# Reordering TensorE's work in a four-layer attention kernel: scores three steps ahead, values in fours, context transposes chained, products held back

## The chip, the cores and the metric

The kernel runs on one core of one Trainium2 chip. The metric is the device time of one execution in microseconds (us). A core has five engines that each work through a queue of their own in order: TensorE (PE in the profile, with its weight loads shown apart as PEld), VectorE (DVE), ScalarE (ACT), GpSimd (POOL) and SyncE (SP), which here issues transfers. They wait for each other through semaphores. TensorE writes into PSUM, eight banks of 2 KB per partition, and the other engines move results on into SBUF. Everything here is 32-bit floating point.

## The reference

The input x is (8, 112, 256): 8 batches of 112 tokens. The context ctx is (8, 375, 192). Four layers follow each other:

```python
# layers 0 and 1: three sub-blocks, each with its own layer norm and a residual
x = attn(ln(x), ln(x)) + x            # self attention, 16 heads of 64, scale 1/8
x = attn(ln(x), ctx) + x              # cross attention over 375 context rows
x = (a * gelu(gate)) @ Wf + bf + x    # a, gate = split(ln(x) @ Wp + bp); 256 -> 2 x 1024 -> 256
# layer 2: cross attention alone, 16 heads of 64
x = x + (softmax(q @ k.T) * scale) @ v @ Wo + bo
# layer 3: decoder block, 16 heads of 16, masks
x = x + self_attn(ln(x), causal and target mask) @ proj_w + proj_b
x = x + cross_attn(ln(x), ctx, context mask) @ out_w + out_b
x = x + gelu(ln(x) @ mlp1_w + mlp1_b) @ mlp2_w + mlp2_b     # 256 -> 1024 -> 256
```

Layer 1 uses the tanh form of gelu, the others the exact one.

## The kernel before

**Stages.** The sub-blocks are numbered as stages: 0, 1, 2 (layer 0: self, cross, feed forward), 3, 4, 5 (layer 1), 6 (layer 2's cross attention), 7, 8, 9 (layer 3: self, cross, feed forward). The 896 tokens lie in seven tiles of 128 rows. The text speaks of three blocks, which the code calls segments 0, 1 and 2: stages 0–2, 3–5 and 6–9. The last block is stage 8 with what is woven into it, and the feed forward behind it (stage 9).

**Steps.** Attention is cut into steps (`add_step`, L913). A self step of stages 0 and 3 takes one batch and 8 of its heads; a cross step one batch and 4 heads; a self step of stage 7 one batch and 8 heads of 16. The 16 self steps of stage 7 are not a run of their own: a dictionary `after` weaves them in pairs between the cross steps of stages 6 and 8. Each step has up to four parts:

- S (`emit_s`): the scores, matmuls at L986 into a PSUM tile `s`. The pool `ps_s` (L313) has two such tiles of two banks each; a cross step and a self step of stage 7 take both, a self step of stages 0 and 3 takes one. The softmax is issued with it. For heads of 64: a maximum on VectorE (L948), one exp per head on ScalarE (L954), a reciprocal (L960, L967) and a scaling on GpSimd (L963 for cross steps, one instruction per head; L969 for self steps). For heads of 16: one VectorE instruction per head adds the mask, copies the scores from PSUM into the SBUF tile `pr` and takes the maximum `nm` (L934); the exps on ScalarE work in `pr` (L942), with the sums collected and divided out once per batch (R and N, L1082–1091).
- E (`emit_late`): for heads of 16, half of the exps are issued with S and the other half here, later in ScalarE's queue.
- T (`emit_t`): transposes of `pr` on TensorE (L1013) into a PSUM tile `mm` (the pool `ps_m`, L314, has four of one bank each), two groups for a self step of 64, three for a cross step (chunks of 128, 128 and 119 context rows). Each group is copied to an SBUF tile `wT`: by ScalarE (L1022) or, for the middle group, VectorE (L1019) in stages 7 and 8; by whichever of the two has less planned load (`evac`, L331; L347 is ScalarE, L355 VectorE) elsewhere.
- PV (`emit_pv`): the values (L1043), accumulated in an `mm` tile that is copied to `oT` (L1054 or `evac`).

**Fillers.** Everything else on TensorE is a filler with a cost and a deadline, counted in steps: key projections (L791 with L800), value projections (L825 with L834; L866 with L875 in stage 8; L750 for self steps), query projections (L703, L725), transposes of the normalized x into `hT` (L637, copied at L642 or by `evac`), products with the output weights (L669, then the residual on VectorE at L673), the transposes of the context into `ctxA` and `ctxB` (L897, six transposes, two copies and one transfer per batch), the feed forward (L1263 in stages 2 and 5, L1298 in stage 9). The class `Plan` keeps them with their dependencies, each with a gap in planned microseconds, and with the room that their results need in SBUF (`arena`, 12224 elements per partition, and rings of weight tiles). `pace` says how much filler work a step must take so that all deadlines are met, `fill` takes the ready one with the earliest deadline, `main` issues a part of a step, `open_jobs` starts a key or value job whose matmul opens early and whose end (`begin` and `fn`) comes in the next step.

**Order.** TensorE's queue is in the order in which the program issues (`manual_schedule` for PE alone); the other engines' order comes from the scheduler, except where `keep_in_program_order` fixes it. So the main loop (L1454–1495) writes TensorE's order out: in step i it issues S(i+2); on every second step PV(i−1) and PV(i); then fillers; the T groups of step i+1 with fillers between them; E(i+2); and fillers again.

**The feed forward at the end.** `last_ff` (L1281) cuts the tokens into 512, 256 and 128 columns (f = 0, 1, 2), with eight products m each. For f = 0 each product (2 matmuls of 512 columns, L1298) has the deadline `ready + 4 + m` in steps, so that they are spread over the last cross steps; their bias is added on the way out of PSUM, and two Gelu instructions over all of them (L1325) come when all eight are there and the last S lies back. For f = 1 VectorE adds the bias (L1309), for f = 2 ScalarE takes bias and Gelu together. Before the first Gelu ScalarE loads another function table (ACT_TABLE_LOAD in the profile). The products L669 of `add_products` with the last weights end the kernel.

Of the kernel before, what the change touches and what calls it, by code (L numbers as in the profile page):

```python
# [299 lines left out]
def kernel(ctx: ExitStack, tc: tile.TileContext, a: dict, out: bass.AP):  # L300
# [3 lines left out]
    ARENA = 12224  # L304
# [4 lines left out]
    ppool = ctx.enter_context(tc.tile_pool(name="ppool", bufs=4))  # L309
    tpool = ctx.enter_context(tc.tile_pool(name="tpool", bufs=6))  # L310
# [235 lines left out]
    def add_masks():  # L546
# [18 lines left out]
        plan.add(Item(("mask", "self"), 0, self_mask, first_of(7, 0) - 8, uses=[src], seg=SEG[6]))  # L565
        yield
        for i in range(2):
            key = ("w", "cm", i)

            def place(i=i, key=key):  # L570
                got[key] = wpool.tile([T, 4, S], F32, tag="w", name="cm")

            plan.add_load(Item(("load", key), 0, place, makes=[key]))
            for n in range(4):

                def ctx_mask(i=i, n=n, key=key):
                    c = B * T + (4 * i + n) * S
                    nc.gpsimd.tensor_scalar_mul(got[key][:, n, :], got[src][:, c : c + S], NEG)

                b = 4 * i + n  # L580
                plan.add(Item(("mask", b), 0, ctx_mask, first_of(8, b) - 5, uses=[src, key], seg=SEG[7]))
# [305 lines left out]
    def add_context_transposes(deadline):  # L887
        for b in range(B):
# [15 lines left out]
            plan.add(Item(("ctxT", b), 0.7, fn, deadline(b), uses=[key], deps=[(("S", 2 + b // 3), 2.0)]))  # L904
# [275 lines left out]
    def q_deadline(st, j):  # L1180
        return first_of(st, 2 * j) - 3.4
# [27 lines left out]
    def hT_by(st):  # L1209
# [4 lines left out]
        return lambda gi: first_of(st, (256 * gi) // T) - 4  # L1214
# [22 lines left out]
    def cross_stage(st, wq, wk, wv, qscale, vscale):  # L1237
# [6 lines left out]
        for b in range(B):  # L1244

            add_key_jobs(st, b, wk, lambda b, u: at[(st, b, u)] - 3.0, last)
# [40 lines left out]
    def last_ff(st, w1, bias):  # L1287
# [3 lines left out]
        for f, (lo, n) in enumerate(LASTG):  # L1291
            ready = last_of(8, last_batch(tiles_of(lo, lo + n)[-1]))
            for m in range(8):

                def fn(f=f, lo=lo, n=n, m=m):
# [12 lines left out]
                    else:  # L1308
                        tc.keep_in_program_order(nc.scalar.activation(dst, ps[:, :n], AF.Gelu, bias=col(bias, m)))  # L1309

                plan.add(
                    Item(
                        ("ff", st, f, m), 8 * n / 2400, fn, ready + (4 + m, 2.5 + 0.2 * m, 5 + 0.1 * m)[f],
                        uses=[w1],
                        deps=h_deps(st, lo, lo + n) + [(("norm", st, t), 0) for t in tiles_of(lo, lo + n)]
                        + ([(("gelu", st, 1), 0)] if f == 2 else []),
# [136 lines left out]

    cuts = [0, ff_at[2], ff_at[5], ff_at[9]]  # L1454
    for seg in range(3):
# [12 lines left out]
        if seg == 0:  # L1468
            plan.require(("hT", 0, 1))
        for i in range(lo - 2, hi):  # L1470
# [6 lines left out]
            if lo <= i + 2 < hi:  # L1477
                plan.main(("S", i + 2))

            if lo <= i < hi and (i - lo) % 2 == 1:  # L1480
                plan.main(("PV", i - 1))
                plan.main(("PV", i))
# [7 lines left out]
            if ("E", i + 2) in plan.items and lo <= i + 2 < hi:  # L1490
                plan.main(("E", i + 2))
# [42 lines left out]
```

## Time and profile before

| what | value |
|---|---|
| median of 3 runs | 1653.15 us (1653.11 to 1653.16) |
| the profiled execution | 1654.93 us |
| its span in the profile | 1653.1 us |
| granted TensorE clock, mean | 0.999 |
| TensorE busy | 1633.3 us in 11772 instructions |
| VectorE, ScalarE, GpSimd busy | 812.8, 782.6, 718.5 us |
| read from HBM, mean over the span | 35.88 MB, 22 GB/s |

A line of the timeline has its start and its duration in us, the engine, the line of the kernel, the operation, result and operand names, the tile sizes, the number of instructions in the group, and in brackets how long the engine stood idle before it and which engine's result ended that wait. A line of the waits has the waiting engine, result and line, the engine, result and line waited for, the total in us, the number of waits and the longest. TensorE's instructions overlap: a matmul's record is longer than the distance to the next one's start, so its busy time is not a measure of how well it is used.

### The profile page before, as it was taken

The numbers are of one execution on the slowest core, as the hardware profiler recorded it, in microseconds if no ns is written. First come the engines' busy times: TensorE is split into PE (matmuls) and PEld (weight loads), VectorE is DVE, ScalarE is ACT, GpSimd is POOL, SyncE is SP. The second block draws the span as 40 slices with busy tenths as digits, with TensorE's granted clock in tenths as the row PEclk, the third lists the DMA queues.
The fourth block names the chain that finished last, engine by engine and source line by source line (L and its number), as shares of the span: only waits on it lengthen the run. The fifth ranks groups of instructions, "written<-read, shape, count | busy, mean of one in ns | idle before, by whom it ended". The sixth has DMA issues, their size and how long they took to land.

```text
span 1653.1 us, 30104 instructions
## 1 busy us (share of the span) xinstructions
PE 1633.3 (99%) x11772; PEld 1141.0 (69%) x11772; DVE 812.8 (49%) x2164; ACT 782.6 (47%) x2450; POOL 718.5 (43%) x687
## 2 busy tenths in 40 slices
PE   9999999999999999999999999999999999999999
PEld 8777766666657878676666665675666666766667
DVE  3554454544532344545444552344455556677752
ACT  3453444444531445434444452144445555787772
POOL 1323555656632223355565570364564447422110
PEclk9999999999999999999999999999999999999999
DMA  6021020000101011000000010100000000000000
GB/s 187 5 66 42 3 87 1 1 26 1 52 29 46 1 29 52 27 1 30 1 2 26 1 46 30 33 23 1 1 2 1 16 2 26 30 2 1 2 2 23
DMA packets 26613, 39.50 MB, mean 24 GB/s; under 512 B 1527, under 2 KB 21623, under 8 KB 26471
## 3 DMA queue, kind: packets, MB, share of 16 engines
q1 hardware_dynamic: 26231, 37.40, 7.3%
q8 instruction: 93, 1.52, 0.4%
q14 instruction: 49, 0.40, 0.1%
q10 hardware_dynamic: 240, 0.17, 0.0%
HBM read 35.88 MB, written 0.92 MB: 22 GB/s over the span
## 4 chain that ended last, share of the span: by engine, by line
PE 91%; ACT 4%; DVE 3%; POOL 1%; issue 1%; ACTq 0%; POOLq 0%; DVEq 0%
PE mm L669 13%; PE mm L703 11%; PE mm L1043 10%; PE s L986 10%; PE mm L1013 9%; PE mm L791 8%; PE mm L825 7%; PE mm L1263 6%; PE mm L800 5%; PE mm L834 4%; PE mm L750 3%; ACT pr L942 2%; PE mm L1298 2%; PE mm L637 1%; ACT pr L954 1%
## 5 line engine op out<-in xcount | busy, mean ns | idle before, releaser
L963 POOL TENSOR_SCALAR pr<-pr,rinv 112x375 f32<-112x375 f32 x384 | 468.7, 1239 | 340.6 <-DVE rinv L960 340.6
L954 ACT ACTIVATE pr<-s,nm 112x375 f32<-112x375 f32 (+1 forms) x640 | 302.0, 490 | 168.7 <-DVE nm L948 166.5
L355 DVE COPY arena<-mm 128x375 f32<-128x375 f32 (+4 forms) x189 | 113.3, 609 | 287.8 <-PE mm L800 138.3
L1013 PEld LDWEIGHTS mm<-ident,pr 112*128 112x128 f32 (+2 forms) x1920 | 209.1, 151 | 48.1 <-issue 20.6
L1013 PE MATMUL mm<-ident,pr 112*128 112x112 f32 (+2 forms) x1920 | 234.7, 264 | 5.5 <-ACT pr L942 3.3
L347 ACT COPY arena<-mm 128x375 f32<-128x375 f32 (+4 forms) x179 | 92.8, 519 | 296.3 <-PE mm L800 140.9
L948 DVE TENSOR_REDUCE nm<-s 112x2 f32<-112x750 f32 (+1 forms) x224 | 206.3, 957 | 50.2 <-PE s L986 46.5
L986 PE MATMUL s<-arena 64*112 64x375 f32 (+3 forms) x1792 | 211.0, 394 | 0.1
L1043 PEld LDWEIGHTS mm<-wT,arena 128*64 128x64 f32 (+5 forms) x3840 | 160.5, 130 | 36.9 <-issue 19.0
L347 ACT COPY wT<-mm 119x448 f32<-119x448 f32 (+2 forms) x235 | 123.9, 536 | 124.5 <-PE mm L1013 124.4
L1043 PE MATMUL mm<-wT,arena 128*64 128x112 f32 (+5 forms) x3840 | 180.3, 262 | 0.0
L986 PEld LDWEIGHTS s<-arena 64*112 64x112 f32 (+1 forms) x1792 | 114.1, 172 | 80.4 <-issue 30.9
L942 ACT ACTIVATE pr<-pr,nm 112x112 f32<-112x112 f32 (+1 forms) x256 | 124.7, 491 | 32.0 <-DVE nm L934 32.0
L969 POOL TENSOR_TENSOR pr<-pr,rinv 112x896 f32<-112x896 f32 x32 | 53.9, 1685 | 197.5 <-DVE rinv L967 180.0
L954 ACT ACTIVATION_READ_ACCUMULATOR pr<-s,nm 112x1 f32 x640 | 133.3, 208 | 0.0
L599 POOL TENSOR_TENSOR rs<-ve,mhalf 128x1 f32<-128x1 f32 x70 | 39.7, 568 | 203.0 <-DVE ve L597 202.9
L960 DVE RECIPROCAL rinv<-sums 112x1 f32<-112x1 f32 x384 | 62.4, 163 | 90.1 <-ACT pr L954 89.6
L825 PE MATMUL mm<-L_xattn_Wv,ctxA 128*128 128x512 f32 (+1 forms) x192 | 92.5, 601 | 2.3 <-ACT wT L347 1.3
L791 PE MATMUL mm<-ctxA,L_xattn_Wk 128*128 128x375 f32 x256 | 92.0, 482 | 0.6 <-DVE wT L355 0.5
L673 DVE TENSOR_TENSOR x<-mm,x 128x256 f32<-128x256 f32 x70 | 29.6, 423 | 115.9 <-PE mm L669 115.9
L703 PE MATMUL mm<-hT,L_xattn_Wq 128*128 128x224 f32 x384 | 83.0, 360 | 0.0
L353 DVE TENSOR_SCALAR arena<-mm 128x448 f32<-128x448 f32 (+2 forms) x65 | 42.0, 646 | 82.0 <-PE mm L834 47.1
(134 smaller groups left out, 2323.7 us busy)
## 6 DMA issues: line engine op xcount, KB each, us to landing
L_xattn_Wo<-in_L_xattn_Wo_dram SPq DMA_DIRECT2D x3, 1024.0 KB, 15.8
L_xattn_w_ff<-in_L_xattn_w_ff_dram SPq DMA_DIRECT2D x3, 1024.0 KB, 5.2
L_xattn_Wv<-in_L_xattn_Wv_dram SPq DMA_DIRECT2D x4, 512.0 KB, 5.0
L_xattn_Wq<-in_L_xattn_Wq_dram SPq DMA_DIRECT2D x2, 1024.0 KB, 4.7
L_xattn_Wp<-in_L_xattn_Wp_dram SPq DMA_DIRECT2D x2, 1024.0 KB, 5.8
L_xattn_wq<-in_L_xattn_wq_dram SPq DMA_DIRECT2D x2, 1024.0 KB
L_xattn_wo<-in_L_xattn_wo_dram SPq DMA_DIRECT2D x2, 1024.0 KB, 5.2
L_xattn_mlp_w<-in_L_xattn_mlp_w_dram SPq DMA_DIRECT2D x2, 1024.0 KB, 5.4
```

The source lines that it names most:

```text
L347: nc.scalar.copy(dst, src)
L669: nc.tensor.matmul(ps[:, :D], lhsT=oT[:, c, t * P : (t + 1) * P], rhs=got[wv or w][:, c, :], start=(c == 0), stop=(c == n - 1),)
L703: nc.tensor.matmul(ps[:, i * 2 * T : (i + 1) * 2 * T], lhsT=got[w][:, k, m * P : (m + 1) * P], rhs=hT[:, k, lo:hi], start=(k == 0), stop=( ...
L791: nc.tensor.matmul(ps[:, :S], lhsT=got[wv][:, (2 * u + i) * P : (2 * u + i + 1) * P], rhs=ctxA[:, cols], start=True, stop=False,)
L825: nc.tensor.matmul(ps[: KCH[c][1], :], lhsT=lhs(ctxA, slice(0, KA), c), rhs=got[w][:, hf * 512 : (hf + 1) * 512], start=True, stop=False,)
L942: return nc.scalar.activation(pr, pr, AF.Exp, bias=nm, scale=-1.0, accum_out=bsums[(st, b)][:, h : h + 1])
L948: nc.vector.tensor_reduce(nm[:, :, :ns], sv, AX.X, ALU.max, negate=True)
L954: nc.scalar.activation(pr[:, bk, sl, :], sv[:, bk, sl, :], AF.Exp, bias=nm[:, bk, sl : sl + 1], accum_out=sums[:, bk, sl : sl + 1],)
L963: nc.gpsimd.tensor_scalar_mul(pr[:, bk, sl, :], pr[:, bk, sl, :], rinv[:, bk, sl : sl + 1])
L986: nc.tensor.matmul(tiles[i][:, n % 2, (n // 2) * nk : (n // 2 + 1) * nk], lhsT=qap(h), rhs=kap(h), start=True, stop=True,)
L1013: nc.tensor.transpose(pt[:kl, m * T : (m + 1) * T], cell[h][:, c * P : c * P + kl], ident[:T, :T])
L1043: nc.tensor.matmul(po[p0 : p0 + dp, blk * T : (blk + 1) * T], lhsT=got[vk][:kl, hv * dp : (hv + 1) * dp], rhs=wt, start=(c == 0 and par(h) ...
```

## The change

Seven things change, all of them in the order and place of instructions:

- The loop keeps a list of S parts that are due. From step `DEEP` on, three steps before the first cross step of stage 8, S is issued three steps ahead in place of two, and E with it. At the step where it begins two S parts follow each other.
- PV parts wait in a list. In segments 0 and 1, for the 16 self steps, they are issued four together on every fourth step; elsewhere two together as before.
- The context transposes of batch b depend on those of batch b − 1, with a gap of 1.5 planned us.
- In `last_ff`, the products m = 5, 6, 7 of f = 0 depend on the last S and get deadlines of `len(steps) − 3` to `len(steps) − 1`.
- The pools of `pr` and `wT` tiles grow from 4 to 6 and from 6 to 8, the arena shrinks from 12224 to 9536 elements.
- Masks are due a step earlier.
- Queries and `hT` of stages 7 and 8, and keys of stage 8, are due a step earlier.

```diff
@@ -301,13 +301,13 @@
     nc = tc.nc
     PSUM = bass.MemoryType.PSUM
     RINGS = {"w": 7, "row": 2, "xn": 3}
-    ARENA = 12224
+    ARENA = 9536
 
     const = ctx.enter_context(tc.tile_pool(name="const", bufs=1))
     wpool = ctx.enter_context(tc.tile_pool(name="wpool", bufs=RINGS["w"]))
     rpool = ctx.enter_context(tc.tile_pool(name="rpool", bufs=RINGS["row"]))
-    ppool = ctx.enter_context(tc.tile_pool(name="ppool", bufs=4))
-    tpool = ctx.enter_context(tc.tile_pool(name="tpool", bufs=6))
+    ppool = ctx.enter_context(tc.tile_pool(name="ppool", bufs=6))
+    tpool = ctx.enter_context(tc.tile_pool(name="tpool", bufs=8))
     xpool = ctx.enter_context(tc.tile_pool(name="xpool", bufs=RINGS["xn"]))
     small = ctx.enter_context(tc.tile_pool(name="small", bufs=4))
     ps_s = ctx.enter_context(tc.tile_pool(name="ps_s", bufs=2, space=PSUM))
@@ -562,7 +562,7 @@
             )
 
         plan.add_load(Item(("load", "masks"), 0, load, makes=[src]))
-        plan.add(Item(("mask", "self"), 0, self_mask, first_of(7, 0) - 8, uses=[src], seg=SEG[6]))
+        plan.add(Item(("mask", "self"), 0, self_mask, first_of(7, 0) - 9, uses=[src], seg=SEG[6]))
         yield
         for i in range(2):
             key = ("w", "cm", i)
@@ -578,7 +578,7 @@
                     nc.gpsimd.tensor_scalar_mul(got[key][:, n, :], got[src][:, c : c + S], NEG)
 
                 b = 4 * i + n
-                plan.add(Item(("mask", b), 0, ctx_mask, first_of(8, b) - 5, uses=[src, key], seg=SEG[7]))
+                plan.add(Item(("mask", b), 0, ctx_mask, first_of(8, b) - 6, uses=[src, key], seg=SEG[7]))
 
 
     xns = {}
@@ -901,7 +901,7 @@
                     evac(dst[:kl, cols], pc[:kl, :S], S)
                 nc.sync.dma_start(ctxB[KB:, cols], ctxB[:KB, cols])
 
-            plan.add(Item(("ctxT", b), 0.7, fn, deadline(b), uses=[key], deps=[(("S", 2 + b // 3), 2.0)]))
+            plan.add(Item(("ctxT", b), 0.7, fn, deadline(b), uses=[key], deps=[(("S", 2 + b // 3), 2.0)] + [(("ctxT", c), 1.5) for c in range(b - 1, b) if b]))
 
 
 
@@ -1178,7 +1178,7 @@
         return lambda t: [(("N", st, last_batch(t)), 1.2)]
 
     def q_deadline(st, j):
-        return first_of(st, 2 * j) - 3.4
+        return first_of(st, 2 * j) - (4.4 if st > 6 else 3.4)
 
     L0 = ("L0_xattn_", "Wq1 Wk1 Wv1 Wo1 bo1 g1 b1 Wq2 Wk2 Wv2 Wo2 bo2 g2 b2 Wp Wf bf g3 b3 bp".split())
     L1 = (
@@ -1211,7 +1211,7 @@
             return lambda gi: last_of(8, last_batch(GROUPS[gi][-1])) + 2.0
         if st in ff_at:
             return lambda gi: ff_at[st] - 0.5 + 0.02 * gi
-        return lambda gi: first_of(st, (256 * gi) // T) - 4
+        return lambda gi: first_of(st, (256 * gi) // T) - (5 if st > 6 else 4)
 
     def norm_by(st):
         f = hT_by(st)
@@ -1243,7 +1243,7 @@
                 add_pair_projection(st, "q", j, wq, 4, lambda j, u: q_deadline(st, j) + 0.01 * u, qscale)
         for b in range(B):
 
-            add_key_jobs(st, b, wk, lambda b, u: at[(st, b, u)] - 3.0, last)
+            add_key_jobs(st, b, wk, lambda b, u: at[(st, b, u)] - (4.0 if last else 3.0), last)
             if not last:
                 add_value_jobs(st, b, wv, lambda b, i: at[(st, b, (0, 0, 2)[i])] - 1.5 + 0.1 * i, vscale)
 
@@ -1308,12 +1308,17 @@
                     else:
                         tc.keep_in_program_order(nc.scalar.activation(dst, ps[:, :n], AF.Gelu, bias=col(bias, m)))
 
+
+
+                held = f == 0 and m > 4
                 plan.add(
                     Item(
-                        ("ff", st, f, m), 8 * n / 2400, fn, ready + (4 + m, 2.5 + 0.2 * m, 5 + 0.1 * m)[f],
+                        ("ff", st, f, m), 8 * n / 2400, fn,
+                        len(steps) - 8.0 + m if held else ready + (4 + m, 2.5 + 0.2 * m, 5 + 0.1 * m)[f],
                         uses=[w1],
                         deps=h_deps(st, lo, lo + n) + [(("norm", st, t), 0) for t in tiles_of(lo, lo + n)]
-                        + ([(("gelu", st, 1), 0)] if f == 2 else []),
+                        + ([(("gelu", st, 1), 0)] if f == 2 else [])
+                        + ([(("S", len(steps) - 1), 0)] if held else []),
                         seg=SEG[st],
                     )
                 )
@@ -1451,6 +1456,7 @@
     nc.vector.tensor_copy(vcols, pt0[:, :NVR])
     plan.now = 7.0
 
+    DEEP = first_of(8, 0) - 3
     cuts = [0, ff_at[2], ff_at[5], ff_at[9]]
     for seg in range(3):
         lo, hi = cuts[seg], cuts[seg + 1]
@@ -1467,6 +1473,7 @@
                     plan.drain(mk)
         if seg == 0:
             plan.require(("hT", 0, 1))
+        waiting = []
         for i in range(lo - 2, hi):
             plan.step = i
             left = plan.pace(i, seg)
@@ -1474,12 +1481,20 @@
 
                 left = max(left, 6.5)
             plan.close_jobs()
-            if lo <= i + 2 < hi:
-                plan.main(("S", i + 2))
-
-            if lo <= i < hi and (i - lo) % 2 == 1:
-                plan.main(("PV", i - 1))
-                plan.main(("PV", i))
+
+
+            ahead = 3 if seg == 2 and i >= DEEP else 2
+            due = [n for n in range(i + 2, i + ahead + 1) if lo <= n < hi and not plan.items[("S", n)].done]
+            for n in due:
+                plan.main(("S", n))
+
+
+            if lo <= i < hi:
+                waiting.append(("PV", i))
+                full = 4 if seg < 2 and i < lo + 16 else 2
+                if len(waiting) == full:
+                    while waiting:
+                        plan.main(waiting.pop(0))
             if lo <= i + 1 < hi:
                 n = steps[i + 1]
                 share = left / (n + 2)
@@ -1487,8 +1502,9 @@
                 for k in range(n):
                     plan.main(("T", i + 1, k))
                     left -= plan.fill(min(left, share))
-            if ("E", i + 2) in plan.items and lo <= i + 2 < hi:
-                plan.main(("E", i + 2))
+            for n in due:
+                if ("E", n) in plan.items:
+                    plan.main(("E", n))
             plan.fill(left, 1.5 if i < lo else 0.0)
 
 
```

## The prediction

> **What bounds the kernel now.** I read the page first, then busy time by stretches, then TensorE's timeline row by row in the last block, then what it waited for, and last the timelines of the engines named there. The page:
>
> ```profile
> PE 1633.3 (99%) x11772; PEld 1141.0 (69%) x11772; DVE 812.8 (49%) x2164; ACT 782.6 (47%) x2450; POOL 718.5 (43%) x687
> ```
>
> TensorE bounds everything, but 99% hides losses: matmul records overlap. Stretches 1400–1600 and 1600–1653 (columns: length, then busy time of PE, PEld, DVE, ACT, POOL, granted clock, DMA share):
>
> ```profile
> 1400.00:1600.00 200.00, 194.06 (x2069) 132.62 (x2068) 144.65 (x565) 148.00 (x477) 54.42 (x82) 1.00 0.03 8
> 1600.00:1653.00 53.00, 47.43 (x334) 40.10 (x331) 17.64 (x51) 18.42 (x39) 5.43 (x7) 0.97 0.06 18
> ```
>
> In the last block TensorE is idle 5.9 of 200 us, the most of any stretch, and ScalarE is busy 148 (74%): the runner-up. TensorE's timeline from the second-last cross step to the feed forward:
>
> ```profile
> 1598.87 0.90 PE L986 MATMUL s<-arena 32*112 32x375 f32 x8
> 1599.70 0.41 PE L1089 MATMUL mm<-ident,rb 112*128 112x112 f32 x2
> 1599.94 0.58 PE L1013 MATMUL mm<-ident,pr 112*128 112x112 f32 x3
> 1600.80 1.12 PE L1013 MATMUL mm<-ident,pr 112*128 112x112 f32 x9 [0.28 <-ACT pr L942]
> 1602.40 1.13 PE L669 MATMUL mm<-squares,oT 128*128 128x256 f32 x4 [0.48 <-ACT wT L1022]
> 1603.46 0.90 PE L986 MATMUL s<-arena 32*112 32x375 f32 x8
> 1604.29 1.36 PE L1043 MATMUL mm<-wT,arena 128*32 128x112 f32 x48
> 1605.59 1.40 PE L1013 MATMUL mm<-ident,pr 112*128 112x112 f32 x12
> ...
> 1613.77 7.20 PE L1298 MATMUL mm<-hT,L_xattn_mlp_w 128*128 128x256 f32 x32 [0.64 <-DVE hT L642]
> ```
>
> Starts tell more than durations. Three transposes from 1599.94 at one per 0.096 us (the x12 group of a quiet step, 1551.19 to 1552.49, gives 0.1) would let the next start at 1600.23; it starts at 1600.80. The printed idle of 0.28 is thus a loss of about 0.57, since the pipe drains and refills. I count every wait by starts. The scores S (L986) are followed too closely by the transposes T of the step before, which need its exps. Waits of TensorE, by cause:
>
> ```profile
> PE mm L1013 <- ACT pr L942: 3.3, 10, 0.7
> ...
> PE mm L791 <- ACT wT L1022: 1.1, 2, 0.6
> ```
>
> ScalarE at the end (exps, copies and Gelu share one queue), GpSimd at the start of the woven steps, and VectorE on a self step's mask and maximum:
>
> ```profile
> 1601.83 0.94 ACT L1022 COPY wT<-mm 128x448 f32<-128x448 f32 x2
> ...
> 1610.63 1.28 ACT L1325 ACT_TABLE_LOAD   x1
> 1611.92 3.71 ACT L1325 ACTIVATE oT<-oT 128x2048 f32<-128x2048 f32 x2
> ```
>
> ```profile
> 1401.27 4.90 POOL L963 TENSOR_SCALAR pr<-pr,rinv 112x375 f32<-112x375 f32 x4
> 1406.11 0.31 POOL L770 MEMSET arena<- 112x256 f32 x1
> 1406.40 4.88 POOL L963 TENSOR_SCALAR pr<-pr,rinv 112x375 f32<-112x375 f32 x4
> ```
>
> ```profile
> 1409.13 0.28 DVE L934 CUSTOM_DVE_ANT_0 pr<-s,cmask 112x112 f32<-112x112 f32 x1 [0.86 <-PE s L986]
> ```
>
> The eighth of these starts at 1410.49 and its accumulator read at 1410.69: 0.195 us each. The span is 1653.1 and the execution 1654.93, 1.8 outside the span and 1.8 above the median 1653.15. I sum against the execution and shift the median by the sum.
>
> **The change, part by part.** No arithmetic is added or removed: every instruction of before is there again in another place, so TensorE's pure work stays and only waits, and changes of tile shape, move. I set TensorE's new instruction order against the old one and laid the rows' start-to-start times along it.
>
> *Values in fours.* Changing TensorE's tile shape costs time: eight S passes run four at a time, 2 x 0.316 = 0.63 by the steps inside the group, but 1603.46 to 1604.29 is 0.83; 48 value passes take 1.14 by their inner steps, but 1604.29 to 1605.59 is 1.30. That is 0.16–0.20 each. The new order has 469 such changes against 478: 9 x 0.18 = −1.6 (ends −0.9 and −1.8). Waits of 0.4–0.6 behind value pairs in block 0 (1-us neighbourhoods of 56.07 and 84.27) mostly go: −0.8 (0 to −1.2). The value outputs only take two PSUM buffers longer together; ppool at 6 and tpool at 8 hold the four steps' tiles, so no buffer wait appears in the order.
>
> *Context transposes* (L897). Each item issues six transposes, two copies and one DMA on SP. Three came in a row with S, a copy and a wait: 169.15 loses 0.63, 214.38 0.90, 237.91 0.85, with restarts 2.75 in all. The copies end 3.5 us after S starts (165.64 to 169.10). The new order spreads the early ones, but three of the S–transposes–T–products groups remain, with 2.84–2.90 us of work where 3.5 is wanted: I take −0.45 (ends 0 and −2.75). Their DMA is 96 kB on a queue whose order is otherwise nearly unchanged, and every weight load is still issued over 17 us ahead: nothing there. If that cover went, the late part of one load (5 us to land) would be the price.
>
> *Masks a step earlier.* Four 1.16-us GpSimd products per half plus 3.5 for the self mask go past an emptier GpSimd (54 of 200 busy): 0; behind them L963 of a cross step would be late by at most 1.2.
>
> *Key and query jobs a step earlier, smaller arena.* In stages 1 and 4, three matmuls that waited 0.40 for a wT copy (3.44 us of work behind an S whose copy is ready 3.84 after it) become key matmuls with 3.22: +0.65 (0 to +1.2). In stage 6 two new waits of the same kind (2.15 us after S: 1.1, and 0.6) come against 1.2 that go: +0.5. There GpSimd too: a step's four scalings take 4.9 us, and the new order puts S's 4.3 and 3.9 us apart in two places, so queueing begins: about 0.6, and 1.6 in place of the 0.35 lost at 1411.33: +1.85. Stage 6 together +2.35 (0 to +4).
>
> *Scores three ahead.* Entry: two S's follow each other directly, the self step's 112-wide and then 375-wide ones, which want the PSUM banks that the eight reduces (8 x 0.195 = 1.56, starting 0.8 after S, 1409.13 against 1408.32) empty: 2.36 after the self S starts, where TensorE is done with it after 0.5. Everything on TensorE queues behind the second S: +1.9 (1.0 to 2.4). Gain: the ten exp waits by starts. Eight before the last S lose 1.12 (near 1460), 0.16, 0.22, 0.82, 0.97, 0.82, 0.54, 0.63 = 5.28. Work between S and its T was 3.4–9 us, a loss where it was under 5, and is now 6–16, mostly 9–12; explicit waits on exps fall from 96 to 8. −5.1 (ends −5.3 and 0).
>
> *What is late next*: the copies of T (L1022). The copies of 1601.83 started when exps queued ahead were out: S 1598.87, wait ended 1602.40, 3.53 later. ScalarE's queue still puts two exps of the new S ahead of the copies. Waits of this kind lose 5.6 us by starts before; the new order has 11 places under 3.3 us with deficits of 4.7, so 0 net, plus 0.4 for restarts within a group (−0.3 to +1.3).
>
> *Held products.* After the last S, TensorE loses 4.05 before (0.37, 0.87, 0.50 at the T's, 0.8 in the values, 1.05 at 1613.77 and the rest small). Three held products, 1.73 each (1566.32 to 1568.05), 5.2 us, fill that. But in ScalarE's queue the table load (1.28) and two Gelus (3.71) now precede three wT copies. With the last S at 0, the first copy ends at 11.0, the Gelus at 16.0, the next copy at 16.5; TensorE wants its PSUM buffer at 14.35: 2.2 lost, 1.05 for hT and the first evacuation, 0.25 restarts: 3.5. Net −0.5 (−4 to +1.5). 1610.63 directly follows the copy that ends at 1610.61: the row shows no wait around the load. The Trainium skill ("ScalarE: Activation LUTs", "What ACT_TABLE_LOAD costs") speaks against the change here: it gives the load about 1283 ns, as the row shows, plus a drain of about 1380 ns, which the rows do not show. By the page the tail would lose 1.4 more and the sum would be −1.8.
>
> Sum: −1.6 −0.8 −0.45 +0.65 +2.35 +1.9 −5.1 +0.4 −0.5 = −3.15 us. Execution 1654.93 to 1651.8, median 1653.15 to 1650.0. A measurement of this kernel tells about 0.2% (3.3 us) from no change.
>
> **The rivals.**
> 1. *The costs are covered.* Entry, GpSimd and Gelu terms (1.9 + 1.85 + about 1) find other work: −3.15 − 4.75 = −7.9, 1645.2. For it: idle GpSimd and VectorE. Against: their waits are on TensorE's own next instruction.
> 2. *Copies take the exps' place.* If exps of the earlier S make copies ready at S + 3.75 rather than 3.53, the 11 places lose about 0.2 each more, with a few new ones 2.5 in all: −0.65, about 1652.5. For it: rows where both waits alternate (1600.80, 1602.40). Against: ScalarE has 26% idle.
> 3. *The lookahead does nothing.* S(i+3) waits for a PSUM tile until its step's reduces are done, and the T waits stay: −3.15 + 5.1 = +1.95, 1655.1. For it: there are only two pairs of score banks. Against: the reduces of the S at 1598.87 have let the first half-exps start by 1600.65, and from S to S lie 4.2 us of work on average.
> 4. *Slower: ScalarE becomes the bound of the last block.* A cross step costs it 4 x 0.59 exps (1600.06 to 1600.65) + 2 x 0.48 copies = 3.3 us against 4.2 of TensorE per step on average, but TensorE's stretches are 1.9–3.3 in about eleven steps. From the point where copies come later than S + 3.9 every step pays, and ScalarE never catches up: 32 x 0.25 = 8.0, and 2 of the 5.1 are lost again: −3.15 + 8.0 + 2 = +6.85, 1660.0. For it: ScalarE's 74% is an average over steps that need 79% (3.3 of 4.2). Against: the last steps, where work is thinnest, still show gaps of 1.51 in its row of exps.
>
> **How the numbers follow.** Forecast 0.35, rival 1 0.20, rival 2 0.12, rival 3 0.08, rival 4 0.25. The forecast's own range is 1647.5 to 1652.5, half of it under 1649.85 where faster begins. Faster: 0.20 + 0.18 = 0.38. Same: 0.17 + 0.12 + 0.07 = 0.36. Slower: 0.25 + 0.01 = 0.26. The range from 1645.0 leaves out half of rival 1 (0.10) and, ending at 1657.5, half of rival 4 (0.12).
>
> **What would show it.** Right: exp waits of L1013 in the last block fall under 1 us; waits on wT by L1022 stay near 5; at the first cross step of the last block S waits for L934's nm for about 1.9; GpSimd's L963 groups join without a gap near 1330 and 1375; after the last S three L1298 512-wide groups, then a wait on wT across the Gelu pair. Wrong: waits on wT well above 6 (rivals 2, 4), or S stalls at every step on nm (rival 3), or no wait at the Gelus (rival 1). A loss in blocks 0 and 1, where I find few new waits, would mean that a queue I costed at nothing was the cover.

## The result and the profile after

| | before | after |
|---|---|---|
| median | 1653.16 us (1653.09 to 1654.79, 6 runs) | 1663.41 us (1661.82 to 1665.41, 6 runs) |
| ratio | | 1.0057, 95% interval 1.0047 to 1.0067 |
| profiled execution, span | 1654.93, 1653.1 us | 1661.82, 1659.4 us |

The change made the kernel 10.25 us slower, where 3.15 us faster was forecast; the range ended at 1657.5. The two profiled executions lie 6.9 us apart and their spans 6.3: the one of before stands 1.8 above its median, the one of after 1.6 below. The six times of the changed kernel fall into two groups, 1661.8 to 1662.0 with a mean granted clock of 0.999 to 1.0, and 1664.8 to 1665.4 with 0.997 to 0.998; the last section comes back to that. The profiled execution of before has a stretch at half clock too, from 1610.28 to 1613.69, which its median has not (columns as in the prediction, the clock third from the end):

```profile
1610.30:1613.60 3.30, 2.83 (x46) 2.10 (x36) 0.70 (x2) 3.27 (x3) 0.00 (x0) 0.50 0.00 0
```

The profiled execution of after has none. At a clock of 1.0 the changed kernel takes 1661.8; the kernel before takes 1652.9 to 1654.4 in the runs beside the experiments. So the change costs 7.4 to 8.9 us at equal clock, and the rest of the 10.25 is clock.

Busy time in the last stretches of the changed kernel (columns as before):

```profile
1400.00:1600.00 200.00, 189.56 (x2009) 130.03 (x2007) 143.47 (x563) 150.72 (x491) 56.65 (x85) 1.00 0.02 8
1600.00:1659.00 59.00, 53.89 (x408) 43.95 (x406) 19.02 (x54) 21.19 (x44) 5.43 (x7) 1.00 0.05 16
```

TensorE is idle 10.4 of 200 us between 1400 and 1600, where it was 5.9. Its waits in the changed kernel:

```profile
PE mm L866 <- ACT wT L1022: 4.7, 5, 2.0
...
PE mm L1298 <- ACT wT L1022: 1.8, 1, 1.8
PE mm L1013 <- POOL pr L963: 1.6, 2, 0.9
...
PE s L986 <- DVE nm L934: 1.1, 1, 1.1
```

One of them in the kernel before:

```profile
PE mm L866 <- ACT wT L1022: 0.7, 3, 0.3
```

The waits of L1013 on the exps of L942, 3.3 us in 10 before, are gone from the list: what the third step was to remove, it removed. In their place stand waits on wT copies, on GpSimd and on the maxima.

Where did the time go? I gave every instruction of TensorE, in its order, its quiet start-to-start distance (0.096 us for 112 columns, 0.216 for 256) and 0.18 per change of tile shape, and subtracted that from the actual starts. What is left over between two points with the same amount of work done is lost time, whether TensorE waited or ran at a lower clock. The stretches are named by the times of before:

| stretch of before, us | lost before | lost after | difference | predicted |
|---|---|---|---|---|
| 0–29 | 2.4 | 2.8 | +0.4 (1.8 to 3.1 in all traces) | 0 |
| 29–111, block 0 | 2.2 | 3.7 | +1.6 | −0.8 |
| 111–272, context transposes | 4.4 | 3.8 | −0.6 | −0.45 |
| 272–931 | 6.5 | 7.6 | +1.1 | +0.65 with the next |
| 931–1223 | 5.3 | 5.1 | −0.2 | |
| 1223–1401, stage 6 | 6.1 | 7.5 | +1.4 | +2.35 |
| 1401–1424, entry | 1.2 | 5.7 | +4.6 | +1.9 |
| 1424–1597, last block | 15.1 | 16.7 | +1.6 | −4.7 |
| 1597 to the end | 5.5 | 3.5 | −2.1 | −0.5 |
| tile shapes, 478 to 469, counted | 84.1 | 82.5 | −1.6 | −1.6 |
| sum | | | +6.3 | −3.15 |

The sum is the difference of the two spans. Between forecast and measurement lie 9.4 us: 6.3 of them in the last block, 2.7 at the entry and 2.4 in block 0, while the tail came out 1.6 better.

But of the 5.5 that the tail loses before, 1.3 is the half-clock stretch. Run 11 below has the same order there at full clock. Before first, then run 11:

```profile
1609.91 2.17 PE L1043 MATMUL mm<-wT,arena 128*32 128x112 f32 x48
1612.02 1.11 PE L637 MATMUL mm<-ident,xn 128*128 128x128 f32 x4
```

```profile
1615.17 1.36 PE L1043 MATMUL mm<-wT,arena 128*32 128x112 f32 x48
1616.47 0.66 PE L637 MATMUL mm<-ident,xn 128*128 128x128 f32 x4
```

By starts the 48 values take 2.11 and 1.30 us, and from L637 to the next L1298 (at 1613.77 and 1617.76) it is 1.75 and 1.29. At equal clock the change gains about 0.8 in the tail, not 2.1.

The entry, TensorE's timeline and GpSimd's in the changed kernel:

```profile
1401.51 1.43 PE L986 MATMUL s<-arena 64*112 64x375 f32 x8
...
1405.64 0.89 PE L986 MATMUL s<-arena 64*112 64x375 f32 x4 [0.22 <-ACT pr L954]
1406.76 0.89 PE L986 MATMUL s<-arena 64*112 64x375 f32 x4 [0.22 <-ACT pr L954]
...
1415.40 0.32 PE L1013 MATMUL mm<-ident,pr 112*128 112x112 f32 x1 [0.90 <-POOL pr L963]
...
1418.89 0.66 PE L986 MATMUL s<-arena 32*112 32x112 f32 x16
1420.62 1.66 PE L986 MATMUL s<-arena 32*112 32x375 f32 x8 [1.06 <-DVE nm L934]
```

```profile
1405.34 4.90 POOL L963 TENSOR_SCALAR pr<-pr,rinv 112x375 f32<-112x375 f32 x4 [1.40 <-DVE rinv L960]
1410.18 0.31 POOL L770 MEMSET arena<- 112x256 f32 x1
1410.47 4.88 POOL L963 TENSOR_SCALAR pr<-pr,rinv 112x375 f32<-112x375 f32 x4
```

The same two S parts before:

```profile
1395.53 1.52 PE L986 MATMUL s<-arena 64*112 64x375 f32 x8
...
1403.01 1.43 PE L986 MATMUL s<-arena 64*112 64x375 f32 x8
```

They lay 7.5 us apart; now, at 1401.51 and 1405.64, it is 4.1. The second has to wait for the exps of the first; GpSimd, which needs 4.9 us for each, ends at 1415.4, and TensorE waits for that. The double S at 1418.89 and 1420.62 comes on top.

Two self steps and a cross step in the last block, TensorE and ScalarE:

```profile
1498.07 0.66 PE L986 MATMUL s<-arena 32*112 32x112 f32 x16
...
1501.29 0.75 PE L986 MATMUL s<-arena 32*112 32x112 f32 x16
...
1505.77 1.13 PE L866 MATMUL mm<-ctx_w,ctxA 128*128 128x256 f32 x4 [1.96 <-ACT wT L1022]
```

```profile
1501.38 0.94 ACT L1022 COPY wT<-mm 128x448 f32<-128x448 f32 x2
...
1505.20 0.94 ACT L1022 COPY wT<-mm 128x448 f32<-128x448 f32 x2
```

Between the copies lie eight exps of a self step, 0.37 us each, one behind the other without a gap. TensorE has the next S 3.2 us after the last one, and ScalarE needs about 3.8 for eight exps and two copies.

Block 0 and the tail of the changed kernel:

```profile
54.65 0.48 PE L897 MATMUL mm<-ident,cn 125*128 125x125 f32 x3
55.58 0.51 PE L897 MATMUL mm<-ident,cn 125*64 125x125 f32 x3 [0.46 <-DVE arena L355]
56.53 0.19 PE L410 MATMUL mm<-ident,brows 8*128 8x8 f32 x1 [0.44 <-PE mm L897]
...
63.67 0.44 PE L637 MATMUL mm<-ident,xn 128*128 128x128 f32 x2 [0.78 <-DVE arena L355]
```

```profile
1613.98 1.28 ACT L1330 ACT_TABLE_LOAD   x1
1615.27 3.71 ACT L1330 ACTIVATE oT<-oT 128x2048 f32<-128x2048 f32 x2
1618.89 1.38 ACT L1022 COPY wT<-mm 119x448 f32<-119x448 f32 x3
```

```profile
1616.96 0.67 PE L1013 MATMUL mm<-ident,pr 112*119 112x112 f32 x4 [0.58 <-DVE oT L1307]
1619.45 3.72 PE L1298 MATMUL mm<-hT,L_xattn_mlp_w 128*128 128x256 f32 x16 [1.82 <-ACT wT L1022]
```

Values in fours leave room in block 0, the plan fills it with a context transpose 22 us earlier than before (54.65 against 76.9), at a place where VectorE has a maximum and four copies from PSUM to do one after the other (53.85 to 56.96). In the tail three copies stand behind the Gelus, as the prediction had it.

### The profile page after: what moved, and what is told of

It reads as the page before. It is cut to its first block, busy times and chain, and to the rows that moved or that the text cites. A ratio compares the mean times of both kernels' runs of the same rounds, so it can differ in the third digit from the quotient of the medians.

```text
span 1659.4 us, 30169 instructions
## 1 busy us (share of the span) xinstructions
PE 1631.8 (98%) x11772; PEld 1141.4 (69%) x11772; DVE 816.6 (49%) x2160; ACT 783.7 (47%) x2454; POOL 718.3 (43%) x687
## 4 chain that ended last, share of the span: by engine, by line
PE 90%; ACT 4%; DVE 3%; POOL 1%; issue 1%; ACTq 0%; DVEq 0%; POOLq 0%
PE mm L669 12%; PE mm L703 11%; PE mm L1043 10%; PE s L986 10%; PE mm L1013 9%; PE mm L791 8%; PE mm L825 7%; PE mm L1263 6%; PE mm L800 5%; PE mm L834 4%; PE mm L750 3%; ACT pr L942 2%; PE mm L1298 1%; ACT pr L954 1%; PE mm L725 1%; DVE pr L934 1%
## 5 line engine op out<-in xcount | busy, mean ns | idle before, releaser
L1013 PEld LDWEIGHTS mm<-ident,pr 112*128 112x128 f32 (+2 forms) x1920 | 208.7, 151 | 45.1 <-issue 20.5
L1013 PE MATMUL mm<-ident,pr 112*128 112x112 f32 (+2 forms) x1920 | 233.3, 263 | 3.7 <-POOL pr L963 1.6
L986 PE MATMUL s<-arena 64*112 64x375 f32 (+3 forms) x1792 | 214.6, 395 | 1.6 <-DVE nm L934 1.1
L347 ACT COPY wT<-mm 128x448 f32<-128x448 f32 (+2 forms) x225 | 118.4, 535 | 109.9 <-PE mm L1013 109.8
L942 ACT ACTIVATE pr<-pr,nm 112x112 f32<-112x112 f32 (+1 forms) x256 | 124.7, 492 | 30.2 <-DVE nm L934 30.2
L791 PE MATMUL mm<-ctxA,L_xattn_Wk 128*128 128x375 f32 x256 | 91.2, 483 | 3.3 <-ACT wT L347 1.8
L355 DVE COPY wT<-mm 128x448 f32<-128x448 f32 (+2 forms) x127 | 77.5, 610 | 16.1 <-PE mm L1013 16.1
```

Of the source, the lines that this page charges most:

```text
L347: nc.scalar.copy(dst, src)
L355: nc.vector.tensor_copy(dst, src)
L791: nc.tensor.matmul(ps[:, :S], lhsT=got[wv][:, (2 * u + i) * P : (2 * u + i + 1) * P], rhs=ctxA[:, cols], start=True, stop=False,)
L986: nc.tensor.matmul(tiles[i][:, n % 2, (n // 2) * nk : (n // 2 + 1) * nk], lhsT=qap(h), rhs=kap(h), start=True, stop=True,)
L1013: nc.tensor.transpose(pt[:kl, m * T : (m + 1) * T], cell[h][:, c * P : c * P + kl], ident[:T, :T])
```

## The experiments

All times are medians; each run has the kernel before beside it on the same chip, with medians from 1653.44 to 1654.11. "The changed kernel" is 1663.41 throughout; it was not run again beside them. The clock divides the times of each kernel into groups, so a median of four runs moves by 1 to 2 us with their mix; where it matters, runs of the same mean clock are compared.

**1. Two steps ahead again.**

```diff
-    ahead = 3 if seg == 2 and i >= DEEP else 2
+    ahead = 2
-    return first_of(st, 2 * j) - (4.4 if st > 6 else 3.4)
+    return first_of(st, 2 * j) - 3.4     # hT, keys and masks likewise
```

> The changed kernel with scores two steps ahead everywhere and with the deadlines of masks, queries, keys and hT as before; fours, context chain, held products and pools stay. Theory A (the third step ahead costs its entry, about 4.5 us between 1405 and 1421 in the changed kernel's trace, and what it saves on exps it loses again on wT copies): the time falls by 4 to 6 us, to about 1658; TensorE's waits on exps (L942) come back to about 3 us of printed idle and its waits on wT copies by L1022 fall from about 7 us to about 3. Rival B (the three-ahead order is neutral and the loss lies in blocks 0 and 1 and the tail): the time stays within 2 us of 1663.

Measured: 1655.86 (10 runs), 1.0014 of before (1.0005 to 1.0023). The third step with its deadlines costs 7.5 us, more than either theory had (7.0 at a clock of 1.0: 1654.8 against 1661.8). The waits of L1013 on L942 are back (2.6 us in 9) and those of L866 on L1022 fall from 4.7 to 0.9; the entry loses 1.15 again, as before the change.

**2. Values in pairs.**

```diff
-    full = 4 if seg < 2 and i < lo + 16 else 2
+    full = 2
```

> The changed kernel with values in pairs everywhere. Theory A (fours leave a hole of a step's values in block 0, which early context transposes fill, whose copies then hold up TensorE at 55.6, 56.5, 57.0 and 63.7: 2.4 us): these four waits go, waits of 0.4 to 0.6 at 56 and 84 come back, and nine tile-shape changes of 0.18 come back: the time falls by 0 to 1 us. Rival B (the chain of the context transposes pulls them forward): the four waits stay and the time rises by 1.6 us.

Measured: 1664.20 (4 runs), 0.8 above the changed kernel and inside its scatter. TensorE's order in block 0 is that of before again up to the first context transpose, and the loss between 29 and 111 falls from 3.7 to 2.15: the fours, not the chain of the transposes, cause it. The nine tile-shape changes are back (84.0), so the fours' gain and their loss cancel.

**3. All exps late.**

```diff
-    for _ in range(len(late) // 2):
+    for _ in range(0):
         late.pop(0)()
```

> The changed kernel with all exps of a 16-wide head step issued in E, behind the copies of the step before, instead of half of them with S; TensorE's order stays. Theory A (with scores three ahead the copies of T stand in ScalarE's queue behind the newer S's first two exps, which wait for its maxima): TensorE's waits on wT copies by L1022 in the last block fall from about 7 us to under 3, waits on exps stay under 1, the time falls by 4 to 6 us. Rival B (ScalarE's total work is the bound there): the same exps are queued, only elsewhere, and the time stays within 1.5 us; waits on exps take the place of those on copies.

Measured: 1662.01 (4 runs), 1.4 less, and the waits of L866 on L1022 are 4.0 us against 4.7: nearer to rival B, though no waits on exps took their place. It is not the place of the newer step's exps in the queue: with all of them behind the copies the next copies wait just as long, because ScalarE has a backlog.

**4. The Gelus behind the last copies.**

```diff
-    deps=[... for m in range(8)] + [(("S", len(steps) - 1), 4.0)],
+    deps=[... for m in range(8)] + [(("T", len(steps) - 1, 2), 0.0)],
```

> The changed kernel with the Gelus of f = 0 and 1 dependent on the last T, so that the three wT copies stand ahead of the table load and the Gelus in ScalarE's queue. Theory A (the loss of 0.6 + 1.8 of printed idle at 1616.96 and 1619.45 is that queue): both waits fall to under 0.5 together and the time falls by 1.5 to 2.5 us. Rival B (the products L669 behind wait for the later Gelus): the wait moves to L669 and the time falls by under 0.5 us.

Measured: 1661.34 (4 runs), 2.1 less. Both waits of the tail are gone, and its loss falls from 3.45 to 1.36. No product waits for a Gelu; L669 has a new wait of 0.7, but on VectorE's oT (L1091). The tail's mechanism is shown.

**5. Short exps made cheap.**

```diff
+    if nk == T:        # self steps of stage 7: one exp over the four heads of a block
+        del late[-len(blk):]
+        late.append(exps)      # scalar.activation over pr as 112 x 448, bias nm[:, 0, 0:1]
```

> The changed kernel, in whose 16 self steps of stage 7 one exp instruction on ScalarE covers the four heads of a block instead of one each, with the first head's maximum; three of four sums are left at one. It leaves out the other heads' own maxima and sums, and 192 of 256 short exps. TensorE's order is the same. Theory A (around woven self steps ScalarE gets three steps' exps within about 6 us of TensorE's work and its backlog holds up the copies): the waits on wT copies by L1022 of L866 fall from 4.7 us of printed idle to under 1.5, the time by 3 to 5 us against 1663. Rival B (the copies are late for their own reasons: PSUM, maxima on VectorE, the place of the copies in the queue): these waits stay above 3.5 and the time falls by under 1.5 us.

Measured: 1656.41 (10 runs), 7.0 less. The wait that was to fall:

```profile
PE mm L866 <- ACT wT L1034: 1.1, 2, 0.8
```

(L1034 is the same copy, moved by the added lines.) TensorE's order is unchanged. Theory A, and more: by the stretches 3.1 of the gain lie between 1449 and 1513 (7.2 lost before this edit, 4.05 with it), where the waits at the three woven places, 0.9, 1.1 and 2.1 by starts, all but vanish, 1.2 at the entry and 0.9 between the two. Another 1.7 lie in stage 6, at 1299.9, where no exp was touched; run 3 shows the same there. I have not followed that up, so about 5.2 of the 7.0 belong to the exps. The same edit on the kernel before was not run: what cheaper exps are worth without the third step stays open.

**6. The entry's second S behind the transposes.**

```diff
-    for n in due:
+    for n in due[:1]:
         plan.main(("S", n))
 ...
+    for n in due[1:]:
+        plan.main(("S", n))
     for n in due:
         if ("E", n) in plan.items:
```

> The changed kernel with the second of the two S parts at the entry issued after the transposes of that step instead of directly behind the first. Theory A (the two S parts in a row cost the entry 1.25 us, as the second waits for the maxima of the first's eight heads): TensorE's wait of 1.06 on nm of L934 goes and the time falls by 0.5 to 1.5 us; the other 3 us of the entry (waits on exps, GpSimd's scaling and wT between 1405 and 1418) stay. Rival B (the entry's loss is all due to the double S): those waits go too and the time falls by 3 to 5 us.

Measured: 1661.95 (4 runs), 1.5 less, at the edge of the scatter. The wait on nm is gone, the one on GpSimd (1.6 us in 2) is not. Theory A.

**7. The old deadlines with three ahead.**

```diff
-    return first_of(st, 2 * j) - (4.4 if st > 6 else 3.4)
+    return first_of(st, 2 * j) - 3.4     # hT, keys and masks likewise; ahead stays 3
```

> The changed kernel with scores three ahead, but with the deadlines of masks, queries, hT and keys of the last stages as before. Theory A (the earlier deadlines take two cross S parts of stage 6 from 7.3 us apart to 3.9, so that exps, GpSimd's 4.9 us of scaling and the copies queue up: 2.4 us between 1405 and 1418): that part of the entry goes, the wait on nm of about 1.1 stays; around the woven steps the S parts lie 0.6 to 1 us further apart and the wT waits shrink by 1 to 2 us; in all the time falls by 2.5 to 4.5 us. Rival B (the third step ahead needs its keys and queries, which now come too late): the time stays within 1.5 us, with new waits of L986 on arena tiles.

Measured: 1661.13 (4 runs), 2.3 less, a little under theory A's range. But these runs have clocks of 0.996 to 0.998; the two at 0.998 (1659.45 and 1660.96) lie about 4.7 under the changed kernel's two at 0.998 (1664.84 and 1665.06). The entry's loss falls from 5.7 to 3.2 with the double S still there, and the L866 waits from 4.7 to 2.7; part of them moves to L791 (2.0). No S waits for a late query or key. So the entry is about half double S and half crowding by the earlier deadlines. The last block loses 1.5 less, too. Of what the third step costs together with its deadlines (run 1), the larger part thus comes with the deadlines, by these few runs.

**8. Lookahead only behind the woven steps.**

```diff
-    DEEP = first_of(8, 0) - 3
+    DEEP = first_of(8, 3) - 2     # with runs 4 and 6, fours in block 1 alone,
+                                  # earlier deadlines only for batches from 3 on
```

> A version meant to beat both: scores three ahead only from two steps before the first cross step of batch 3, behind the last woven self steps, with the earlier deadlines only for what these steps need, the second S of the entry behind the transposes, the Gelus behind the last T, fours only in block 1. Theory A (the lookahead hurts only where ScalarE and GpSimd are crowded, and gains where plain cross steps follow each other): entry and woven waits stand as before the change, exps waits after 1510 fall by 3 us, the tail loses 4 us less than before, tile shapes 0.7 us less: 1646 to 1650. Rival B (the copies take the place of the exps in the plain cross steps too): 1650 to 1654.

Measured: 1654.25 (11 runs), 1.0002 of before (0.9993 to 1.0011). That is rival B by the time, just above its range. Of the 4.2 us that the tail gains here beside the profile of before, 1.3 is that one's half-clock stretch; all of the rest is given back: 0.6 between 459 and 931, 1.0 in stage 6 and 1.8 in the last block, where waits on wT (0.9 at 1520.6) and on hT (1.3 at 1531.7) now stand.

**9. The held products alone, on the kernel before.**

```diff
-    ready + (4 + m, 2.5 + 0.2 * m, 5 + 0.1 * m)[f],
+    len(steps) - 8.0 + m if f == 0 and m > 4 else ready + (...)[f],
+    deps += [(("S", len(steps) - 1), 0)] if f == 0 and m > 4
```

> The kernel before with only the held products: m = 5, 6, 7 of f = 0 depend on the last S and are due in the last three steps. With scores two steps ahead ScalarE's queue still has all wT copies ahead of the table load. Theory A (the three products fill the 4 us that TensorE loses behind the last S, and their old places did not need them): the time falls by 2.5 to 4.5 us against 1653.2 to 1654.0, faster than both kernels. Rival B (in their old places they covered the exps of the last steps): waits of L1013 on L942 near 1590 to 1600 grow by what the tail gains, and the time falls by under 1 us.

Measured: 1652.46 (11 runs), 0.9989 of before (0.998 to 0.9998): faster than both kernels, by 1.65 us against the kernel before on its chip (1.2 against its runs at a clock of 1.0, which all 11 runs have here; each of the 11 is under all 18 of before). Both theories hold in part: the tail loses 1.37 in place of 5.54, of which 1.3 was clock, but the last steps, which the three products left, lose 7.86 in place of 6.28 (waits on exps near 1589 and 1596).

**10. The new sizes alone, on the kernel before.**

```diff
-    ARENA = 12224      # ppool 4, tpool 6
+    ARENA = 9536       # ppool 6, tpool 8
```

> The kernel before with only the new sizes: pr tiles 6, wT tiles 8, arena 9536. From 179 to 1344 us of TensorE's work the order of key, value and query jobs changes with the smaller arena. Theory A (the smaller arena brings the losses of about 0.5 us between 460 and 930 and 1.0 to 1.4 between 1220 and 1400 us, where jobs stand behind late wT copies): the time rises by 1 to 2 us against the kernel before. Rival B (fours in block 1 and the other changes bring them): the time stays within 0.5 us.

Measured: 1658.90 (7 runs), 1.0032 of before (1.002 to 1.0043): 4.8 us, more than twice what theory A had.

**11. The arena alone.**

```diff
-    ARENA = 12224
+    ARENA = 9536
```

> The kernel before with only the arena at 9536 elements; pr and wT tiles stay at 4 and 6. TensorE's order is nearly that of the run with all three new sizes. Theory A (the arena is the cause: with less room, key and value jobs are opened at other steps, S parts of stage 6 come closer together and GpSimd's scaling queues up): the time rises by 3.5 to 6 us against the kernel before, with the waits of L1013 on L963 near 1370. Rival B (the added tiles change when buffers come free): under 1 us.

Measured: 1658.78 (5 runs), 1.003 of before (1.0018 to 1.0042): 5.3 us, and 4.0 between the two profiled spans (1657.1 and 1653.1), which have one half-clock stretch each. The tiles play no part. TensorE and GpSimd in stage 6 of this kernel:

```profile
1367.58 1.52 PE L986 MATMUL s<-arena 64*112 64x375 f32 x8
1369.03 0.41 PE L1013 MATMUL mm<-ident,pr 112*128 112x112 f32 x2
1370.14 0.32 PE L1013 MATMUL mm<-ident,pr 112*128 112x112 f32 x1 [0.70 <-POOL pr L963]
1371.35 1.12 PE L1013 MATMUL mm<-ident,pr 112*128 112x112 f32 x9 [0.89 <-POOL pr L963]
```

```profile
1366.44 9.70 POOL L963 TENSOR_SCALAR pr<-pr,rinv 112x375 f32<-112x375 f32 x8 [2.19 <-DVE rinv L960]
```

With less room the value job that stood between two S parts of the kernel before (1360.89 and 1367.92, 7.0 apart) comes later; they are now 1363.60 and 1367.58, GpSimd gets eight scalings in a row, and the transposes wait 2.05 by starts. Right behind it TensorE runs at half its clock, in the stretches' view of this kernel:

```profile
1372.80:1375.90 3.10, 3.10 (x5) 1.27 (x4) 0.40 (x2) 0.00 (x0) 3.10 (x3) 0.50 0.00 0
```

That costs 1.6 more. With it stage 6 loses 8.7 in place of 6.1, and 272 to 1223 another 1.9.

**12. Held products and lookahead for the last eight steps, with the old sizes.**

```diff
+    DEEP = first_of(8, 6) - 2     # loop as in run 6, Gelus as in run 4, held products as in run 9
+                                  # ppool stays at 4, and all else as before
```

> The kernel before with the held products, the Gelus behind the last T, and scores three ahead only from two steps before batch 6 of stage 8, the second S of the entry behind the transposes; sizes, deadlines, pairs and context transposes as before. Theory A (in the last eight steps ScalarE has room, so the waits of L1013 on L942 of 1.25 us by starts near 1589 and 1596 go, at no price at the entry): 0.8 to 1.5 us below the kernel with the held products alone (1652.5), so near 1651.3. Rival B (four pr tiles let S go ahead but not its maxima, and the copies take the exps' place): within 0.7 us of it or above.

Measured: 1665.36 (6 runs), 1.0062 of before (1.0047 to 1.0076), 12.9 above run 9; its two runs at a clock of 1.0 (1660.2 and 1660.71) are about 8 above it, and the rest is clock. Rival B, far beyond its number. TensorE, VectorE, and the stretch behind:

```profile
1578.00 0.97 PE L1013 MATMUL mm<-ident,pr 112*128 112x112 f32 x8
1580.20 1.82 PE L986 MATMUL s<-arena 32*112 32x375 f32 x8 [1.23 <-DVE nm L934]
```

```profile
1579.13 0.54 DVE L934 CUSTOM_DVE_ANT_0 pr<-s,cm 112x375 f32<-112x375 f32 x1
```

```profile
1582.70:1585.60 2.90, 2.90 (x8) 1.67 (x7) 1.19 (x4) 0.53 (x1) 0.67 (x2) 0.50 0.00 0
```

The S whose maximum this is started at 1571.75. Its maxima start only at 1579.13, when the transposes of the step that held the pr tiles are through (1578.00 + 0.97); the next S waits for them. The copy L1019 just ahead of them in VectorE's queue waits for the same transposes, so these rows do not part the tiles from the queue. The count does: a cross step fills two pr tiles, so four hold two steps, and with four a third step ahead has nowhere to put its scores. Six are needed. At their largest a pr tile takes 896 elements and a wT tile 448; two more of each are 2688, just what the arena gives up, and run 11 is the bill. With six pr and the old six wT tiles the arena could keep 10432; that, and whether the third step needs eight wT tiles at all, was not run.

## Why the prediction was wrong

**"ppool at 6 and tpool at 8 hold the four steps' tiles", the arena in "+0.65" and "+2.35".** The mechanism was named, jobs moved and S parts too close for GpSimd, but I credited it to the key and query deadlines and priced it by two places in TensorE's order. Alone on the kernel before the arena costs 5.3 us, 1.6 of it by the clock (run 11), where I had 3.0 for both terms. In the full change the same stretches lose 2.3 more, so there the size was right and the source mistaken: runs 1 and 7 put the deadlines back, and the loss between 272 and 931 stays within 0.1 us. What the arena alone is worth inside the full change no run shows.

**"Entry: +1.9 (1.0 to 2.4)".** It was 4.6. The double S loses 1.25 (run 6 takes it away); most of the rest (2.5 by run 7) is two cross S parts that the earlier deadlines drew together, a step that I had costed only for its direct effect on queues, not for what stands between one S and the next. The sum had the crowding in stage 6 alone; run 7 shows another 1.5 of it in the last block.

**"Explicit waits on exps fall from 96 to 8. −5.1" and "0 net" for the copies.** The first is right, and the second is the step that failed: waits on wT copies came in the exps' place (those of L866 grew from 0.7 to 4.7 us of printed idle), and the last block lost 1.6 more where the sum had 4.7 less. I had the copies' release from a quiet cross step (S + 3.53) and ScalarE's load as an average, 3.3 of 4.2 us per step. At the woven steps it gets two self steps of eight exps and a cross step within 6.3 us of TensorE's time. Run 3 shows that the queue's order is not the point; run 5, which takes work from ScalarE and leaves TensorE's order as it is, points to the amount of work. That is rival 4's engine, but not its place: not every cross step pays, three woven places do.

**"Waits in block 0 mostly go: −0.8".** +1.6. I looked for waits that the fours remove, and not for what the plan would put into the gap (run 2).

**Tail, −0.5.** The mechanism is right, nearly to its size (2.2 worked out, 1.99 measured by starts; 1.05 worked out for the other, 0.74 measured), and run 4 shows it. The gain that the products bring was undersized by 1.6, and its base was misread: the 4.05 that TensorE loses behind the last S held the half-clock stretch ("0.8 in the values" and part of the 1.05), as the clock of 0.97 in the row for 1600 to 1653 could have told. The median, to which I shifted the sum, does not have that stretch. Without it my own terms give a loss of about 0.8 in the tail, where 0.8 was gained at equal clock. The Trainium skill's page "ScalarE: Activation LUTs", section "What ACT_TABLE_LOAD costs", adds a drain of about 1380 ns to the load of about 1283. Here the load runs from 1613.98 to 1615.26 and the Gelu starts at 1615.27, and the copy ahead of the load ended at 1613.96: the load agrees, no drain is seen.

**Tile shapes −1.6, transposes −0.45.** Both hold (−1.6 by the order, −0.6 measured). The chain alone was not tried.

Nothing in the sum stood for the loss of clock behind waits, which makes some of them dearer than they look. Undoing the third step gives 7.5, the arena alone 5.3, the fours −0.8 and the held products −1.65: 10.4 together, beside the 10.25 measured. These prices come from different kernels and clocks, and the arena's is 2.3 in the full change; that they add up so well is luck.

## What to carry to other kernels

When work is moved earlier, look at the distance between the pieces that feed the slower engines, not at the distance between a piece and its user: an engine that is three quarters busy on average can be behind for ten microseconds at a place where three feeds come together. A deeper lookahead needs its buffers, and if these come out of the space by which a planner orders everything else, measure the planner with less space alone first. Fill a gap at the end with held work only if it is not the cover of the steps that it is taken from.

## What the runs showed of the hardware

TensorE's clock falls to half behind waits far shorter than I had thought to count. The traces record the granted clock. After the start and before the last microseconds the 14 traces have 15 stretches at 0.50, in which start-to-start distances double (256 columns in 0.427 us against 0.216). Thirteen last 3.41 us, one 6.83 (run 6) and one 10.24 (run 12): one, two and three times 3.413. Each begins a whole number of 3.413 us after the first switch to full clock in its trace. A stretch of 3.41 us can lose 1.7 us of work; in the tail of before it lost 1.3.

In none of the 3.41 us in front of the 15 was TensorE idle throughout: the records of its matmuls cover 39 to 73% of them. A long wait alone is not enough: the same wait of 1.25 us at the entry is followed by half clock in runs 2 and 4 and not in the profiled execution of the changed kernel. Where the wait lies in the raster of 3.413 us differs between them. What amount of work keeps the clock up, these runs do not show.

That accounts for the two groups of times as well: two stretches, a mean clock of 0.998, lose up to 2 x 1.7 = 3.4 us, and the groups lie 3.1 apart. The Trainium skill's page "TensorE: Matmul & The Clock Gate", section "What's actually happening", gives half clock after at least one idle window of about 3.4 us that runs free of the kernel. The length of the stretches and their raster agree with such a window; that the whole of it must be idle does not, by the 39 to 73%.
